# A graph layer on one core: four neighbouring nodes to a partition, and the mixer's projections made in the gather stage

## The chip, the core and the metric

The kernel runs on one core of one Trainium2 chip. The metric is device time in microseconds. The core has five engines that work side by side and wait for one another through semaphores: TensorE (PE in the profile; PEld is its weight load), VectorE (DVE), ScalarE (ACT), GpSimd (POOL) and SyncE (SP), which here only issues DMAs. Each engine takes its instructions in order. GpSimd issues the indirect DMAs that gather table rows.

## The reference

A layer of a graph network over 6250 nodes of 256 features and 206,250 edges, in float32. `xn` is the layer norm of `x`. Three parts follow: graph attention over the edges, a linear-attention mixer over all nodes, and a mixture of eight experts over the normed sum. Cut to what matters here:

```python
xn = _layernorm(x)
# graph attention: x1 = xn @ W, 64 wide; four heads
e = exp(leaky_relu((x1 @ Wl.T)[src] + (x1 @ Wr.T)[dst], 0.2))
w = e / segment_sum(e, src)[src]
gnn = elu(segment_sum(w[:, h] * x1[dst], src) + b)      # for each head h
# mixer: 4 heads of 32
q, k, v = split(rmsnorm(xn, g_pre) @ w_qkv)
k, v = with the 4 memory columns mem_kv put ahead
q = softmax(q, over the 32 of a head) * 32 ** -0.5
k = softmax(k, over all nodes)
mix = rmsnorm((k^T v applied to q) @ w_out + b_out, g_out) + xn
y = x + gnn + mix
out = y + layernorm(y) + sum over the top 2 of 8 experts of gelu(..w1..) w2
```

The softmax of `k` runs over all nodes, so the mixer's small matrix `cw` (`k^T v`, scaled, times `w_out`) is known only when every node's key and value have been seen. Nothing of the mixer enters the graph attention; both meet in `y`.

## The kernel before

Nodes are taken in 49 tiles of 128 (`NT`), the last with 106. Node `128 t + p` lies in tile `t` on partition `p`. Tiles are handled in 13 `groups` of up to four (`GT`). PSUM is shared out in small pools; the ones that matter are `mps` in the first part, and `hps` (one buffer, `h_ps`) and `yps` (two buffers, `y_ps`) later.

**The front.** `load_edges()` (L201) brings the ids of source and destination; lines 244 to 255 cut them into a tile-pair number (`bid`) and two values of a few bits (`va`, `vb`). Then `project()` (L303) is called for each group. It loads four tiles of `x`, takes mean and variance on ScalarE (L309, L315), normalises (L338), transposes on TensorE (L343), copies back (L345) and multiplies with `wcat`, 456 columns: 384 for queries, keys and values, 72 for what the graph attention needs (L348). ScalarE evacuates the product in three pieces: queries to `q_all` (L351), keys and values to `kv` (L352), and the 72 columns to `tab` (L355), which is stored to the DRAM `table`. After each group come three calls of `sort_batch()` (L370), 39 of its 51; it sorts 32 x 128 edges by tile pair with one-hot products, of which the largest operation is the one-hot `ohp` on VectorE (L448). The other 12 batches follow, and between them the steps of `context()` (L467): the maximum of all keys (L468), its spread over the partitions, and for each group a subtraction on GpSimd (L498), an exponential on ScalarE (L499) and one matmul a tile that adds to `ctx_ps` (L502). It ends with `cw` (L521).

**The gather stage.** A loop over blocks of tiles (L1082 and on) does for every tile: `weights()` (L1016), which makes the edges' weights from the gathered rows `xe`; four times `sums()` (L1035), whose one-hot `ohw` (L1041) and matmuls into `a_ps` (L1048) add up a quarter's edges; between them `look()` (L980) for the next tile and a part of `pack()` (L875), which puts a pair of tiles' edges in order and calls `gather()` (L969). That issues 35 indirect DMAs a tile from GpSimd, one a column, into one of three `xe` buffers; a buffer is free again when its tile's sums are done.

**What fills the loop.** Generators in `todo` give up one step at a time. `some_more()` (L1058) is called after each quarter and takes steps until their costs reach `FC` = 2. At first `todo` holds `attention()` (L574): three steps of cost 2 for each group, which turn the queries into the mixer's output and store `base_y`. When it is used up, the experts' weights are loaded, and `finish_steps()` (L661) of each block follows: ELU, norm, routing, and for 8 experts the hidden products (L775), Gelu (L783), the second products (L791) and their weighted addition (L795).

The order of instructions on each engine is laid out by a planner from dependencies and program order. `later()` (L567) adds a dependency, without a semaphore, on the first gather's indices, so that an instruction isn't placed ahead of the gather stage.

The lines of the order in which work is given out:

```python
for t0, n in groups:
    project(t0, n)
    for _ in range(3):
        sort_batch(batches.pop(0))
...
todo = [(attention(), [FC] * (3 * len(groups)))]
```

Of the kernel before, what the change touches and what calls it, by code (L numbers as in the profile page):

```python
# [1 line left out]

# [6 lines left out]
F32 = mybir.dt.float32  # L9
F16 = mybir.dt.float16  # L10
BF16 = mybir.dt.bfloat16
I32 = mybir.dt.int32
# [5 lines left out]
P = 128  # L18
# [17 lines left out]
def tile_gps_layer(  # L36
# [37 lines left out]
    last = N - (NT - 1) * P  # L74
    EC = -(-NE // P)
# [14 lines left out]
    KW = 2 * HID + 1  # L90
    O_TAB = 3 * HID
    O_EL = O_TAB + H + FO
    PW = O_EL + H
    assert NPAD > N and PW <= 512 and last > 0
# [72 lines left out]

    def load_rows(dst_tile, source, t0, n, rows):
        full = n if (t0 + n) * P <= rows else n - 1
        if full < n:  # L170
            nc.vector.memset(dst_tile[:, full, :], 0.0)
        if full:
            nc.sync.dma_start(
                out=dst_tile[:, :full, :],
                in_=source[t0 * P:(t0 + full) * P, :].rearrange("(t p) d -> p t d", p=P),
            )
        if full < n:
            r = rows - (t0 + full) * P
            nc.sync.dma_start(out=dst_tile[:r, full, :], in_=source[(t0 + full) * P:rows, :])
# [21 lines left out]
    def load_edges(pool):  # L201
        return load_ids(pool, "src_i", src, NB * U * P), load_ids(pool, "dst_i", dst, N)
# [33 lines left out]
    with tc.tile_pool(name="ids", bufs=1) as lp:  # L236
# [21 lines left out]
    nc.scalar.dma_start(out=wcat[:, :, :3 * HID], in_=w_qkv.rearrange("(c p) f -> p c f", p=P))  # L258
    nc.scalar.dma_start(
        out=wcat[:, :, O_TAB + H:O_EL], in_=gnn_W.rearrange("(c p) f -> p c f", p=P)  # L260
    )
# [3 lines left out]
    gpre = kp.tile([P, DC], F32, name="gpre")  # L265
# [5 lines left out]
    wo = kp.tile([P, D], F32, name="wo")  # L271
    nc.scalar.dma_start(out=wo, in_=w_out)
    mk = kp.tile([P, NM], F32, name="mk")
    nc.scalar.dma_start(out=mk, in_=mem_kv[0].rearrange("h d m -> (h d) m"))
    mv = kp.tile([P, NM], F32, name="mv")
# [6 lines left out]
    for c in range(DC):  # L282
        wt_ps = mps.tile([FO, P], F32, name="tp")
        nc.tensor.transpose(wt_ps, wcat[:, c, O_TAB + H:O_EL], ident)
        wT = qw.tile([FO, P], F32, name="wT")
        nc.scalar.copy(wT, wt_ps)
        wlr_ps = mps.tile([P, 2 * H], F32, name="pr")
        nc.tensor.matmul(wlr_ps, lhsT=wT, rhs=lrT, start=True, stop=True)
        nc.scalar.copy(wcat[:, c, O_TAB:O_TAB + H], wlr_ps[:, :H])
        nc.scalar.copy(wcat[:, c, O_EL:PW], wlr_ps[:, H:])  # L290
        nc.vector.tensor_scalar(
            wcat[:, c, :3 * HID], wcat[:, c, :3 * HID], gpre[:, c:c + 1], None, op0=OP.mult
        )

    q_all = qp.tile([P, NT, HID], F32, name="q_all")
    kv = kp.tile([P, NT, KW], F32, name="kv")
    nc.gpsimd.memset(kv[:, :, KW - 1:KW], 1.0)
    kmax = kp.tile([P, HID], F32, name="kmax")
# [4 lines left out]
    def project(t0, n):  # L303
# [10 lines left out]
        for j in range(n):  # L314
# [8 lines left out]
        rn = qw.tile([P, GT], F32, name="rn")  # L323
        nc.scalar.activation(rn[:, :n], var, AF.Sqrt, scale=float(D))
        nc.vector.tensor_mul(rn[:, :n], rn[:, :n], rs)
        nc.vector.tensor_scalar_max(rn[:, :n], rn[:, :n], 1e-12)
        nc.vector.reciprocal(rn[:, :n], rn[:, :n])
        nc.vector.tensor_scalar_mul(rn[:, :n], rn[:, :n], float(D) ** 0.5)
        shift = qw.tile([P, GT], F32, name="shift")
        nc.vector.scalar_tensor_tensor(  # L330
            shift[:, :n], stats[:, t0:t0 + n, 0], -1.0, rs, op0=OP.mult, op1=OP.mult
# [3 lines left out]
        for j in range(n):  # L335
# [3 lines left out]
                xn, xt[:, j, :], AF.Identity, bias=shift[:, j:j + 1], scale=rstd[:, t:t + 1]  # L339
# [7 lines left out]
            for c in range(DC):  # L347
# [3 lines left out]
            nc.scalar.activation(q_all[:, t, :], pr[:, :HID], AF.Copy, scale=rn[:, j:j + 1])  # L351
            nc.scalar.activation(  # L352
                kv[:, t, :2 * HID], pr[:, HID:3 * HID], AF.Copy, scale=rn[:, j:j + 1]
            )
            nc.scalar.copy(tab[:, j, :], pr[:, O_TAB:PW])  # L355
        nc.gpsimd.tensor_copy(el[:, t0:t0 + n, :], tab[:, :n, TW - 1:])
        nc.gpsimd.memset(tab[:, :n, TW - 1:TW], 1.0)
        nc.sync.dma_start(
            out=table[t0 * P:(t0 + n) * P, :].rearrange("(t p) f -> p t f", p=P),
            in_=tab[:, :n, :TW],  # L360
        )
# [104 lines left out]

    def context():  # L467
        nc.vector.tensor_reduce(  # L468
            kmax, kv[:, :NT - 1, :HID].rearrange("p t d -> p d t"), axis=AX.X, op=OP.max
        )  # L470
        nc.vector.tensor_max(kmax[:last], kmax[:last], kv[:last, NT - 1, :HID])
        km_ps = mps.tile([HID, P], F32, name="tp")
        nc.tensor.transpose(km_ps, kmax, ident)
        kcol = kp.tile([P, 2], F32, name="kcol")
        nc.vector.tensor_reduce(kcol[:, 0:1], km_ps, axis=AX.X, op=OP.max)
        nc.vector.tensor_reduce(kcol[:, 1:2], mk, axis=AX.X, op=OP.max)
        kmc = kp.tile([P, 1], F32, name="kmc")
        nc.vector.tensor_max(kmc, kcol[:, 0:1], kcol[:, 1:2])
        kr_ps = mps.tile([P, HID], F32, name="tp")
        nc.tensor.transpose(kr_ps, kmc.to_broadcast([P, P]), ident)  # L480
        krow = kp.tile([P, HID], F32, name="krow")
        nc.vector.tensor_copy(krow, kr_ps)
        nkm = kp.tile([P, 1], F32, name="nkm")
        nc.vector.tensor_scalar_mul(nkm, kmc, -1.0)
        emk = kp.tile([P, NM], F32, name="emk")
        nc.scalar.activation(emk, mk, AF.Exp, bias=nkm)
        mm_ps = mps.tile([NM, 2, P], F32, name="tp")
        nc.tensor.transpose(mm_ps[:, 0, :], emk, ident)
        nc.tensor.transpose(mm_ps[:, 1, :], mv, ident)
        memT = kp.tile([NM, 2, P + 1], F32, name="memT")  # L490
        nc.vector.memset(memT, 1.0)
        nc.vector.tensor_copy(memT[:, :, :P], mm_ps)
        ctx_ps = mps.tile([P, HID + 1], F32, name="pr")
        nc.tensor.matmul(ctx_ps, lhsT=memT[:, 0, :P], rhs=memT[:, 1, :], start=True, stop=False)
        yield
        for t0, n in groups:
            kk = kv[:, t0:t0 + n, :HID]
            nc.gpsimd.tensor_sub(kk, kk, krow[:, None, :].to_broadcast([P, n, HID]))  # L498
            nc.scalar.activation(kk, kk, AF.Exp)  # L499
            for t in range(t0, t0 + n):  # L500
                rows = P if t < NT - 1 else last
                nc.tensor.matmul(  # L502
                    ctx_ps, lhsT=kv[:rows, t, :HID], rhs=kv[:rows, t, HID:KW],
                    start=False, stop=(t == NT - 1),
                )
            yield
        rden = kp.tile([P, 1], F32, name="rden")
        nc.vector.reciprocal(rden, ctx_ps[:, HID:HID + 1])
        nc.vector.tensor_scalar_mul(rden, rden, float(DH) ** -0.5)
        cbd = kp.tile([P, HID], F32, name="cbd")  # L510
        nc.vector.memset(cbd, 0.0)
        for h in range(MH):
            s = slice(h * DH, (h + 1) * DH)
            nc.vector.tensor_scalar(cbd[s, s], ctx_ps[s, s], rden[s], None, op0=OP.mult)
        cT_ps = mps.tile([P, HID], F32, name="tp")
        nc.tensor.transpose(cT_ps, cbd, ident)
        cT = kp.tile([P, HID], F32, name="cT")
        nc.scalar.copy(cT, cT_ps)
        cw_ps = mps.tile([P, D], F32, name="pr")
        nc.tensor.matmul(cw_ps, lhsT=cT, rhs=wo, start=True, stop=True)  # L520
        nc.scalar.copy(cw, cw_ps)  # L521
        yield

# [6 lines left out]
    nc.sync.dma_start(out=eltab.rearrange("(t p) h -> p t h", p=P), in_=el)  # L530
# [13 lines left out]
    steps = context()  # L544
    while batches:
        sort_batch(batches.pop(0))
        next(steps, None)
    for _ in steps:
        pass
# [23 lines left out]

    def attention():  # L574
# [4 lines left out]
        for t0, n in groups:  # L579
# [10 lines left out]
            o_g = qw.tile([P, GT, D], F32, name="o_g")  # L590
            ss = qw.tile([P, GT], F32, name="ss")
            for j in range(n):
# [7 lines left out]
                sq = qw.tile([P, D], F32, name="sq")  # L600
# [9 lines left out]
            for j in range(n):  # L610
# [9 lines left out]
            nc.sync.dma_start(  # L620
                out=base_y[t0 * P:(t0 + n) * P, :].rearrange("(t p) d -> p t d", p=P),
                in_=xt[:, :n, :],
            )
# [37 lines left out]
    def finish_steps(hps, yps, x2, t0, n, rows_left, gb, more=None):  # L661
# [8 lines left out]
        def rows_at(t, k):  # L670
            return slice(t * P, (t + k) * P) if isinstance(t, int) else bass.ds(t * P, k * P)

        def front():
            yt = fw.tile([P, GT, D], F32, name="yt")
            nc.sync.dma_start(
                out=yt[:, :n, :],
                in_=base_y[rows_at(t0, n), :].rearrange("(t p) d -> p t d", p=P),
            )
# [121 lines left out]
        def store():  # L800
            full = n if rows_left is None else n - 1
            if full:
                nc.sync.dma_start(
                    out=out[rows_at(t0, full), :].rearrange("(t p) d -> p t d", p=P),
                    in_=x2[:, :full, :],
                )
            if full < n:
                nc.sync.dma_start(out=out[(NT - 1) * P:N, :], in_=x2[:rows_left, n - 1, :])
# [455 lines left out]
```

## Time and profile before

| | us |
|---|---|
| three runs | 4218.44, 4218.94, 4224.91 (median 4218.94) |
| the profiled execution | 4182.5 |
| its span, from first to last instruction | 4180.7 |
| first gather issued | 446.22 |
| last gather issued (last column's start) | 3993.6 |

| engine | busy us | share of the span | instructions |
|---|---|---|---|
| PE | 2268.6 | 54% | 15401 |
| PEld | 1663.9 | 40% | 15401 |
| DVE | 1919.8 | 46% | 3941 |
| ACT | 746.2 | 18% | 1653 |
| POOL | 1669.8 | 40% | 1774 |

How to read the profile's lines: in a row of slices, each digit is the busy share of a fortieth of the span in tenths; PEclk is the granted TensorE clock in tenths. A group of instructions reads: line, engine, operation, output and inputs, shape, count, then busy time in us and mean ns of one, then the engine's idle time just before them and what ended it. A row in order of time reads: start, duration, engine, line, operation, names, count, and in brackets the idle time before it with what ended it. A row of a stretch of time gives its length, then busy time and count for PE, PEld, DVE, ACT and POOL, the granted clock as a share of one, the share of the DMA engines and GB/s. A wait ended by "remote" is one whose end the profile can't put down to an instruction.

### The profile page before, as it was taken

What the parts mean: (1) busy time and instruction counts of PE and PEld (TensorE: products, weight loads), DVE (VectorE), ACT (ScalarE), POOL (GpSimd) and SP (SyncE); (2) the same over time, 40 slices, a digit from 0 to 9 for tenths busy, and PEclk for the clock granted to TensorE, in tenths of its full rate; (3) what the DMA queues carried; (4) which work ended last, traced back from release to release, by engine and by line L of the source; (5) the groups of instructions that cost most, each with busy time, mean ns of one, the idle gap of its engine ahead of it and who ended that gap; (6) DMA issues with size and microseconds to landing.
All of it is one profiled execution on the core that took longest, in us unless ns stands there. A gap on an engine that the chain in (4) does not pass through costs nothing. (4 is left out here: it accounts for less than half of the span.)

```text
span 4180.7 us, 39357 instructions
## 1 busy us (share of the span) xinstructions
PE 2268.6 (54%) x15401; PEld 1663.9 (40%) x15401; DVE 1919.8 (46%) x3941; ACT 746.2 (18%) x1653; POOL 1669.8 (40%) x1774
## 2 busy tenths in 40 slices
PE   7877232435254764644765555455364573554677
PEld 4544232324242543433543433334253352442456
DVE  7787444536352443533442523425343452342423
ACT  5542001212111111111111110111111111110122
POOL 1001545454445344344344344544535335344410
PEclk8875555666666877776877776777676686776778
DMA  1020111111121111011011100101101001011100
GB/s 59 28 29 1 21 28 41 37 41 37 34 74 20 22 19 23 18 24 22 12 29 18 25 17 17 30 17 22 25 12 27 18 19 25 13 25 19 23 12 7
DMA packets 106548, 103.75 MB, mean 25 GB/s; under 512 B 42678, under 2 KB 78740, under 8 KB 106356
## 3 DMA queue, kind: packets, MB, share of 16 engines
q0 software_dynamic: 54720, 60.52, 8.4%
q1 hardware_dynamic: 49940, 39.75, 3.3%
q8 instruction: 123, 2.02, 0.2%
q10 hardware_dynamic: 1696, 0.89, 0.1%
q14 instruction: 69, 0.57, 0.0%
HBM read 86.39 MB, written 14.65 MB: 24 GB/s over the span
## 5 line engine op out<-in xcount | busy, mean ns | idle before, releaser
L972 POOL DMA_INDIRECT xe<-table,dst_x x1710 | 1635.7, 957 | 2011.0 <-PE a_ps L1048 1323.2
L1048 PE MATMUL a_ps<-ohw,xe 128*65 128x128 f32 x4400 | 665.1, 307 | 235.7 <-issue 189.3
L1048 PEld LDWEIGHTS a_ps<-ohw,xe 128*65 128x65 f32 x4400 | 590.8, 159 | 314.4 <-issue 243.1
L775 PE MATMUL h_ps<-tokT,w1s 128*128 128x512 f32 (+3 forms) x896 | 442.8, 610 | 235.1 <-ACT hT L783 205.1
L795 DVE SCALAR_TENSOR_TENSOR x<-y_ps,comb,x 128x256 f32<-128x256 f32 x392 | 187.0, 481 | 782.4 <-remote 479.1
L791 PE MATMUL y_ps<-w2s,hT 128*128 128x256 f32 x1568 | 436.7, 413 | 147.6 <-issue 107.2
L791 PEld LDWEIGHTS y_ps<-w2s,hT 128*128 128x128 f32 x1568 | 315.5, 208 | 273.0 <-issue 177.5
L940 PE MATMUL s_ps<-rc,ohp 128*128 128x144 f16 x2525 | 255.1, 260 | 279.5 <-DVE ohp L935 146.8
L1041 DVE TENSOR_TENSOR ohw<-oh,bank 128x1280 f32<-128x1280 bf16 x196 | 321.5, 1641 | 170.1 <-remote 149.3
L940 PEld LDWEIGHTS <-ohp 128*128 128x128 f16 x2525 | 209.6, 114 | 324.2 <-DVE ohp L935 162.9
L1009 PE MATMUL e_ps<-elw,ohT 128*128 128x48 bf16 x588 | 36.2, 199 | 544.7 <-ACT ohT L1001 477.8
L783 ACT ACTIVATE hT<-h_ps,b1s 128x512 f32<-128x512 f32 (+3 forms) x224 | 140.4, 627 | 1018.4 <-remote 531.0
L775 PEld LDWEIGHTS h_ps<-tokT,w1s 128*128 128x128 f32 x896 | 171.8, 214 | 345.7 <-ACT hT L783 226.0
L1001 ACT COPY ohT<-t_ps 128x768 bf16<-128x768 bf16 x98 | 78.3, 799 | 1130.1 <-remote 842.3
L930 DVE TENSOR_TENSOR rc<-ohc,bank 128x1152 f16<-128x1152 f16 (+1 forms) x350 | 231.2, 687 | 64.8 <-remote 62.2
L1009 PEld LDWEIGHTS <-ohT 128*128 128x128 bf16 x588 | 27.0, 106 | 577.2 <-ACT ohT L1001 505.9
L935 DVE TENSOR_TENSOR ohp<-to,bank 128x2048 f16<-128x2048 f16 (+1 forms) x175 | 193.5, 1105 | 0.0
L763 PE MATMUL y_ps<-b2s,cTs 8*128 8x256 f32 x98 | 49.7, 600 | 192.4 <-ACT cTs L761 118.6
L764 DVE TENSOR_TENSOR x<-x,y_ps 128x256 f32<-128x256 f32 x49 | 20.6, 420 | 269.7 <-remote 164.6
L1018 DVE TENSOR_REDUCE z<-e_ps 128x140 f32<-128x420 f32 (+1 forms) x49 | 28.7, 585 | 244.6 <-PE e_ps L1009 224.1
L923 DVE TENSOR_TENSOR ohc<-to,bank 128x1152 f16<-128x1152 f16 (+1 forms) x175 | 119.6, 683 | 0.3 <-ACT to L911 0.2
L448 DVE TENSOR_TENSOR ohp<-rank,iota_h 128x4096 f16<-128x4096 f16 (+1 forms) x51 | 116.1, 2277 | 6.3 <-ACT rank L439 6.0
(273 smaller groups left out, 2568.0 us busy)
## 6 DMA issues: line engine op xcount, KB each, us to landing
xe<-table,dst_x POOLq DMA_INDIRECT x1710
xt<-in_x_dram SPq DMA_DIRECT2D x24, 512.0 KB
base_y<-xt SPq DMA_DIRECT2D x12, 512.0 KB
yt<-base_y SPq DMA_DIRECT2D x9, 512.0 KB
out_dram<-x SPq DMA_DIRECT2D x9, 512.0 KB
w1s<-in_L_ffn_w_dram SPq DMA_DIRECT2D x8, 256.0 KB
w2s<-in_L_ffn_w_dram SPq DMA_DIRECT2D x8, 256.0 KB
table<-tab SPq DMA_DIRECT2D x12, 138.0 KB
```

The costliest lines, as they stand in the source:

```text
L448: nc.vector.tensor_tensor(pairs(ohp[:, :w]), two(rank2[:, :w], P // 2), row(iota_h, P // 2), op=OP.is_equal)
L775: nc.tensor.matmul(h_ps[:, :w], lhsT=w1s[:, e, c, f * P:(f + 1) * P], rhs=held["tokT"][:, c, :w], start=(c == 0), stop=(c == DC - 1),)
L783: nc.scalar.activation(held[e][:, f, :w], h_ps[:, :w], AF.Gelu, bias=b1s[:, k:k + 1])
L791: nc.tensor.matmul(y_ps, lhsT=held[e][:, f, j * P:(j + 1) * P], rhs=w2s[:, e, f, :], start=(f == 0), stop=(f == FC - 1),)
L795: results.append(nc.vector.scalar_tensor_tensor(x2[:, j, :], y_ps, held["comb"][:, j, e:e + 1], x2[:, j, :], op0=OP.mult, op1=OP.add,))
L923: nc.vector.tensor_tensor(pairs(ohc[:, :m]), twos(to[:, 0, t0:t0 + m], U * CW // 2), iota_2[:, :, :U * CW // 2].to_broadcast([P, m, U * CW ...
L930: nc.vector.tensor_tensor(pairs(rc[:, :m, i, :]), pairs(ohc[:, :m]), twos(edges_q[:, t0:t0 + m, i, :], U * CW // 2), op=OP.mult,)
L935: nc.vector.tensor_tensor(pairs(ohp[:, :m]), twos(to[:, 1, t0:t0 + m], P // 2), iota_2.to_broadcast([P, m, P // 2, 2]), op=OP.is_equal,)
L940: nc.tensor.matmul(flat(s_ps), lhsT=ohp[:, t - t0, :], rhs=flat(rc[:, t - t0]), start=(t == 0), stop=(t == NBT - 1),)
L972: nc.gpsimd.indirect_dma_start(out=xe[:, c, :], out_offset=None, in_=table, in_offset=bass.IndirectOffsetOnAxis(ap=dst_x[:, c:c + 1], axis=0),
L1041: nc.vector.tensor_tensor(ohw[:, :n], oh[:, g0:g1, i, None, :].to_broadcast([P, n, H, SN]), ew_s[:, c0:c0 + n, :, None].to_broadcast([P, n ...
L1048: nc.tensor.matmul(a_ps[:, i].rearrange("f h n -> f (h n)"), lhsT=xe[:, c, H:], rhs=ohw[:, c - c0].rearrange("p h n -> p (h n)"), start=(c ...
```

## The change

Two things are done at once.

**The layout.** Of the first 48 tiles (`NF`), four make a block of 512 nodes, and node `512 g + 4 p + t` now lies on partition `p` of tile `4 g + t`: four neighbouring nodes share a partition, one in each of four tiles. The last tile stays as it was. `pieces()` gives the matching views of a DRAM tensor, and `load_rows()` and a new `store_rows()` use it for `x`, `table`, `base_y` and `out`; a group of four tiles is then one run of four rows in DRAM for each partition. The source ids are renumbered to fit in `load_edges()`, with five VectorE operations over 128 x 1612. The tables in DRAM keep the nodes' order, so the destination ids and the gathers' indices stay as they are.

**The projections.** `project()` keeps only the 72 columns for the graph attention; it also keeps the norm's scale and shift of every tile in `rn_all` and `shift_all`. Queries, keys and values move to a new `context()`, a generator in `todo` ahead of `attention()`. For each group it loads `x` again, normalises with both norms' factors in one ScalarE operation, transposes, and projects: the keys transposed, 128 x 512 for four tiles, the queries and values a tile at a time. In place of one maximum over all nodes it holds a running one: a single number a feature, raised group by group, and `sums_c` is shrunk by `exp(old - new)` before a group's `k^T v` is added. The costs of the steps become 1 each, 80 in all. Some buffers of `attention()` go from two to one (`o_g`, `sq`). The store of `eltab`, which only the overflow branch at the end reads, moves into that branch.

The diff, cut to its core:

```diff
+    NF = N // (GT * P) * GT
+    def pieces(dram, t0, n, rows):
...
+            if t < NF:
+                e = min(t0 + n, g + GT)
+                ap = dram[g * P:(g + GT) * P, :].rearrange("(p t) f -> p t f", t=GT)
+                found.append((t - t0, e - t0, P, ap[:, t - g:e - g, :]))
...
     def load_edges(pool):
-        return load_ids(pool, "src_i", src, NB * U * P), load_ids(pool, "dst_i", dst, N)
+        src_i, dst_i = load_ids(pool, "src_i", src, NB * U * P), load_ids(pool, "dst_i", dst, N)
...
+        nc.vector.scalar_tensor_tensor(
+            part, src_i, float(NF * P), src_i, op0=OP.is_lt, op1=OP.mult
+        )
+        nc.vector.tensor_single_scalar(turn, part, GT - 1, op=OP.bitwise_and)
+        nc.vector.tensor_scalar(
+            part, part, 2, P - 1, op0=OP.logical_shift_right, op1=OP.bitwise_and
+        )
+        nc.vector.scalar_tensor_tensor(
+            src_i, turn, float(P - 1), src_i, op0=OP.mult, op1=OP.add
+        )
+        nc.vector.scalar_tensor_tensor(
+            src_i, part, -float(GT - 1), src_i, op0=OP.mult, op1=OP.add
+        )
...
     def project(t0, n):
...
-            nc.scalar.activation(q_all[:, t, :], pr[:, :HID], AF.Copy, scale=rn[:, j:j + 1])
-            nc.scalar.activation(
-                kv[:, t, :2 * HID], pr[:, HID:3 * HID], AF.Copy, scale=rn[:, j:j + 1]
-            )
-            nc.scalar.copy(tab[:, j, :], pr[:, O_TAB:PW])
+            nc.scalar.copy(tab[:, j, :], pr)
...
-    steps = context()
     while batches:
         sort_batch(batches.pop(0))
-        next(steps, None)
...
+    def context():
...
+        xt = load(0)
+        yield
+        for g, (t0, n) in enumerate(groups):
+            v = vs[g % 2]
+            xnT = qw.tile([P, DC, GT * P], F32, name="xnT", bufs=1)
+            for j in range(n):
+                t = t0 + j
+                xn = xn_of()
+                nc.scalar.activation(
+                    xn, xt[:, j, :], AF.Identity, bias=shift_all[:, t:t + 1],
+                    scale=rn_all[:, t:t + 1],
+                )
+                xT_ps = yps.tile([P, DC, P], F32, name="y_ps")
+                for c in range(DC):
+                    nc.tensor.transpose(xT_ps[:, c, :], xn[:, c * P:(c + 1) * P], ident)
+                nc.scalar.copy(xnT[:, :, j * P:(j + 1) * P], xT_ps)
+            if g + 1 < len(groups):
+                xt = load(g + 1)
+            yield
...
+            k_ps = hps.tile([P, GT * P], F32, name="h_ps")
+            for c in range(DC):
+                nc.tensor.matmul(
+                    k_ps[:, :w], lhsT=wqvk[:, c, 2], rhs=xnT[:, c, :w],
+                    start=(c == 0), stop=(c == DC - 1),
+                )
+            here = small("here")
+            nc.vector.tensor_reduce(here, k_ps[:, :w], axis=AX.X, op=OP.max)
+            new = small("most")
+            nc.vector.tensor_max(new, most, here)
+            less = small("less")
+            nc.vector.tensor_scalar_mul(less, new, -1.0)
+            shrink = small("shrink")
+            nc.scalar.activation(shrink, most, AF.Exp, bias=less)
+            most = new
+            ekT = qw.tile([P, GT * P], F32, name="ekT", bufs=1)
+            nc.scalar.activation(ekT[:, :w], k_ps[:, :w], AF.Exp, bias=less)
+            for j in range(n):
+                qv_ps = yps.tile([P, 2, HID], F32, name="y_ps")
+                for c in range(DC):
+                    nc.tensor.matmul(
+                        flat(qv_ps), lhsT=xnT[:, c, j * P:(j + 1) * P],
+                        rhs=flat(wqvk[:, c, :2]), start=(c == 0), stop=(c == DC - 1),
+                    )
+                nc.scalar.copy(q_all[:, t0 + j, :], qv_ps[:, 0])
+                nc.scalar.copy(v[:, j, :HID], qv_ps[:, 1])
+            yield
+            ek_ps = yps.tile([P, GT, P], F32, name="y_ps")
...
+                nc.tensor.transpose(ek_ps[:r, j, :], ekT[:, j * P:j * P + r], ident)
...
+            nc.scalar.copy(ek[:r, :n], ek_ps[:r, :n])
+            c_ps = yps.tile([P, HID + 1], F32, name="y_ps")
+            for j in range(n):
+                nc.tensor.matmul(
+                    c_ps, lhsT=ek[:r, j, :], rhs=v[:r, j, :], start=(j == 0), stop=(j == n - 1)
+                )
+            nc.vector.scalar_tensor_tensor(
+                sums_c, sums_c, shrink, c_ps, op0=OP.mult, op1=OP.add
+            )
+            yield
...
-    todo = [(attention(), [FC] * (3 * len(groups)))]
+    todo = [(chain(context(), attention()), [1] * (6 * len(groups) + 2))]
```

## The prediction

> **What bounds the kernel now.** I read the page first, then the groups of instructions by line (shapes kept apart), the order of time inside one gather, and last a table of busy time by stretch. On the page, these rows count:
>
> ```profile
> PE   7877232435254764644765555455364573554677
> POOL 1001545454445344344344344544535335344410
> PEclk8875555666666877776877776777676686776778
> L972 POOL DMA_INDIRECT xe<-table,dst_x x1710 | 1635.7, 957 | 2011.0 <-PE a_ps L1048 1323.2 <-issue 595.6 <-PE y_ps L594 57.8
> ```
>
> No engine is full after the first tenth. GpSimd gathers 1710 columns at 957 ns and otherwise waits, mostly for `a_ps`: the sums of a node tile free the `xe` buffer that the next gather writes. A gather is 35 columns, one each 1.25 us (starts 3592.22, 3593.47), so about 44 us; 49 of them are 2140 us of the 4181. A node tile takes longer than that, and the order of time says why:
>
> ```profile
> 3604.23 0.69 PE L791 MATMUL y_ps<-w2s,hT 128*128 128x256 f32 x2 [0.34 <-issue]
> 3604.73 0.94 POOL L972 DMA_INDIRECT xe<-table,dst_x  x1 [0.30 <-issue]
> ...
> 3634.73 0.95 POOL L972 DMA_INDIRECT xe<-table,dst_x  x1 [0.30 <-issue]
> 3641.49 0.58 ACT L783 ACTIVATE hT<-h_ps,b1s 128x384 f32<-128x384 f32 x1 [44.30 <-remote]
> 3641.49 0.48 DVE L795 SCALAR_TENSOR_TENSOR x<-y_ps,comb,x 128x256 f32<-128x256 f32 x1 [30.11 <-remote]
> 3642.13 1.65 PE L775 MATMUL h_ps<-tokT,w1s 128*128 128x384 f32 x2 [37.21 <-ACT hT L783]
> ```
>
> The gather began at 3592.22. For some 12 us the other engines work beside it; then ScalarE waits 44.3 us and VectorE 30.1 us for products that TensorE had finished by 3605, and all go on some 6 us after the last column was issued. So the later two thirds of a gather hide hardly any work that passes between engines. What a tile needs beyond those first 12 us stands behind the gather. The first part of the kernel, before any gather (first at 446.22), is another matter:
>
> ```profile
> L448 DVE TENSOR_TENSOR ohp<-rank,iota_h 128x4096 f16<-128x4096 f16 x50 | 115.2, 2303 | 6.1 <-ACT rank L439 6.0
> L348 PE MATMUL pr<-wcat,xT 128*128 128x456 f32 x196 | 109.8, 690 | 5.9 <-ACT xT L345 5.9
> L468 DVE TENSOR_REDUCE kmax<-kv 128x128 f32<-128x6144 f32 x1 | 11.0, 11044 | 0.0
> ```
>
> ```profile
> core 0: us, PE busy (x) PEld busy (x) DVE busy (x) ACT busy (x) POOL busy (x), PEclk, DMA share, GB/s
> ...
> 200.00:250.00 50.00, 43.92 (x482) 25.57 (x482) 38.30 (x61) 29.16 (x111) 0.61 (x4) 0.77 0.09 28
> 350.00:400.00 50.00, 36.62 (x516) 26.31 (x516) 39.14 (x55) 5.85 (x28) 0.00 (x0) 0.57 0.01 1
> ...
> 558.78:1238.70 679.92, 271.68 (x1852) 223.99 (x1851) 330.97 (x690) 101.19 (x234) 339.98 (x351) 0.64 0.18 41
> 1238.70:1774.90 536.20, 315.21 (x1786) 222.61 (x1784) 238.22 (x513) 89.33 (x132) 234.16 (x245) 0.75 0.12 25
> 2018.80:3201.30 1182.50, 635.10 (x3739) 468.51 (x3738) 479.77 (x1002) 155.59 (x229) 534.70 (x561) 0.72 0.11 21
> ```
>
> While project() runs (200 to 250), TensorE is busy 88% and paces the sort; where sorting is alone (350 to 400), VectorE leads at 78%. The last three rows go from gather start to gather start: 10 tiles with attention as their extra work, 7 with the experts' backlog, 16 in steady state.
>
> **An exchange rate.** Per tile they last 68.0, 76.6 and 73.9 us, with PE, DVE and ACT busy 70.4, 91.8 and 79.4 us in sum. From the first row to the second, 21.4 us more work cost 8.6 us, a rate of 0.40; to the third, 9.0 us cost 5.9, a rate of 0.65. I price work moved into the gather stage so.
>
> **Front, removed.** `pr` shrinks from 456 to 72 columns, two ACT evacuations a tile go (L351 0.364, L352 0.467 us), three small DVE operations a group, the 11.0 us `kmax`, the GpSimd subtraction, the exponential and 98 context matmuls. None of this is on the path by itself: the sort's 51 batches are. Their L448 start at 36.6 and end with 410.0, 50 steps of 7.47 us. With sorting alone (377.77, 384.69, 391.61, 398.53) a step is 6.92. I take that pace for all: 50 x 0.55 = 28 us won. Ends: VectorE's own work in a batch is 6.05 us (L448 2.30, L427 1.02, L444 1.21, L387 0.62, L412 0.59, L399 0.27), with the loop's small operations 6.45, which wins 51; a lighter but still interleaved project() at 7.4 wins 4.
>
> The row shows 0.77 granted clock with project() and 0.57 without, at 88% and 73% TensorE. The Trainium skill, "TensorE: Matmul & The Clock Gate", section "Part 1: The HAM clock gate", says that the array idles at half clock and only sustained work opens it; so thinning TensorE's work would take back part of the gain. By that rule the pace stays at the 6.92 of the half-clock stretch, 28 us; by a clock held at 0.77, up to 51.
>
> **Front, added.** load_edges() renumbers the source nodes: three scalar_tensor_tensor over 128x1612 (L252, 1.83 us) and two tensor_scalar (L248, 1.00), 7.5 us on VectorE between the arrival of the indices (6.4 us) and the first batch. Nothing hides it but TensorE's first projections, which get shorter too: +7.5, ends 0 and 7.5.
>
> **Gather stage, added.** Each group of four tiles now needs, by the nearest rows (busy time over count). On PE, 4 matmuls of 512 columns (L775, 0.494) for keys, 16 of 256 (L791, 0.279) for queries and values, 12 transposes (L343, 0.247), 8 of 129 (L502, 0.186): 2.0 + 4.5 + 3.0 + 1.5 = 11.0 us. On ACT, 4 normalisations (L338, 0.606), 4 copies (L345, 0.385), the shrink factor (0.30, as L321), the exponential (0.634, as L499), 8 copies of queries and values (0.264, as L596), the copy of `ek` (0.58, as L1106): 7.6 us. On DVE, a maximum over 512 (0.68, as L583), two small ones (0.15 each), the update of `sums_c` (0.29, as L482): 1.3 us.
>
> That is 19.9 us, times 12.25 groups (49 tiles) 244 us. At 0.40 it costs 98 us; at 0.65, 158. I take 0.40, the rate of the busiest stretch, since these tiles are as loaded. The lower end is 0, if the gathers hide it after all.
>
> Where the work falls: two cost units a call and one a step now, so 80 steps in 40 calls; tiles 0 to 5 carry 2.7 groups of context each, tiles 5 to 10 2.7 of attention where there were 1.3. The total of attention is unchanged, and the experts start at the same tile; at one rate this moves nothing, and the other rate is in the range. The waits it adds are ACT's for `y_ps` (two buffers, shared with heads and experts). Queued behind them on ACT are the `ohT` copies of look(), on which TensorE's `e_ps`, then `z` and the next tile's sums wait.
>
> **DMAs.** 13 more loads of x on SP (0.37 us to issue), each a group ahead of its use, covered by two more steps; without that cover a load would be seen in full, as the 8 us from 7.17 to the first use at 15.36. Nothing is added on GpSimd's queue. The `eltab` store moves behind a branch not taken: 0, SP was idle. Four rows to a partition make longer pieces of x, base_y, table and out. None of these transfers is on the path; they can only slow a gather's columns, whose mean is 957 ns against 944 undisturbed: 1710 x 13 ns = 22 us at most to win, and with 13 loads more on some 37, 8 to lose. I take 0.
>
> **Sum.** -28 + 7.5 + 98 = +78 us on the profiled 4182.5 (span 4180.7): 4260. The three runs shown have a median of 4218.94, 36 above the profiled one; I carry the difference over: 4297 us, slower by 1.8%. Its own range, from the ends: 98 - 51 + 0 - 22 = +25 to 158 - 4 + 7.5 + 8 = +170, so 4244 to 4389.
>
> **The rivals**, each with its time at the level of the median.
>
> **The gathers hide it.** The change's 244 us run inside the idle two thirds of the gathers, at no price: 4219 - 28 + 7.5 = 4198, faster. For it: TensorE is at 40% in the first ten tiles, and now and then it does run a whole quarter of sums late in a gather. Against: the stall at 3605, and that attention's work already shows in the period. It decides if less than 20 of the 244 us shows. Chance 0.19.
>
> **Handing over is what costs.** A group passes 16 times between TensorE and ScalarE where attention passes 8 times, and each passage that falls into a gather may wait for its end. At 0.65 or above: 4219 - 20 + 158 = 4357; at 1.0, 4443. For it: in the view of waits, ScalarE's `ohT` copies stand 842 us in all. Against: the heaviest stretch has the lower rate. Chance 0.20.
>
> **It doesn't move.** The planner could draw the projections back into the front; then TensorE, at 88%, pays again and only 7.5 us is sure: about 4226 and up. Against: the added gates let nothing begin before the first gather's indices. Chance 0.03.
>
> **It cancels** to within the noise, with a gather price near 20 us: 4219. Chance 0.05.
>
> **How the numbers follow.** The forecast holds 0.53, and 4297 is its value. Slower by over 0.2%: 0.53 + 0.20 + 0.03, less 0.01 that ends level = 0.75. Within 0.2% (8 us, about what a measurement of this kernel can tell from no change): 0.06. Faster: 0.19. The range 4190 to 4395 takes in the likeliest's own range, the level cases, most of the first rival and half of the second; 0.10 is left out on either side.
>
> **What would show it.** Right: the first gather starts near 426 instead of 446; the L448 of the new kernel step at 6.9; tiles 0 to 5 last some 80 us instead of 68; from tile 11 on the periods are as before. Wrong: a front no shorter (then the sort's own chain paces it), a first gather before 400, tiles 0 to 5 still at 70 (the first rival), or at 95 and more (the second). A change of the period in steady state would mean that the layout matters, which I cost at nothing.

## The result, and the profile after

The changed kernel takes 4261.89 us (median of 4, 4255.28 to 4272.14) beside 4220.51 us before: ratio 1.0106, 95% interval 1.0087 to 1.0126. It is slower by 41 us; 78 were forecast. The profiled execution is one of the four (4272.14 us). That of before (4182.5) lay 38 us under its median, so the two profiles are compared by place, not by their ends.

Rows of the page of the changed kernel, the same as were shown of before:

```profile
PE   6876244644344666464655554455364473554577
POOL 1000654454545334435344345444535335344410
PEclk9999567767676777686777776777677686776778
...
L1043 POOL DMA_INDIRECT xe<-table,dst_x x1710 | 1631.1, 954 | 2143.1 <-PE a_ps L1119 1426.4
```

A column still takes 954 ns (957 before); GpSimd waits 1426 us for the sums, where it waited 1323. The first gather starts at 425.6 us (446.22 before). The one-hots of the sort (now L474) start at 38.8 and the last one at 389.4: 50 steps of 7.01 us, where they were 7.47. The table of busy time by stretch, from gather start to gather start (to 0.1 us), the same tiles as the three rows shown of before:

```profile
541.10:1274.40 733.30, 348.90 (x2309) 278.29 (x2309) 336.76 (x716) 153.90 (x442) 337.41 (x351) 0.70 0.16 41
1274.40:1834.70 560.30, 322.23 (x1776) 228.31 (x1777) 249.13 (x550) 90.53 (x138) 232.39 (x246) 0.72 0.14 31
2070.40:3275.60 1205.20, 634.01 (x3763) 467.46 (x3762) 482.36 (x1006) 158.29 (x232) 535.36 (x561) 0.72 0.10 20
```

Counted from 0, tiles 2 to 11 last 53 us longer, with 136 us more work on PE, DVE and ACT; the next seven 24 longer with 19 us more, and the 16 steady ones 23 longer with 4 us more. What the context costs the engines, from the groups of instructions between 425 and 1300 us (line, engine, operation, count, then busy us and mean ns):

```profile
L620 PE MATMUL y_ps<-wqvk,xnT 128*128 128x256 f32 x196 | 59.9, 447 | 95.4 <-remote 51.1 <-ACT v L625 37.1 <-ACT xnT L595 6.5
L588 ACT ACTIVATE xn<-xt,shift_all,rn_all 128x256 f32<-128x256 f32 x49 | 28.8, 603 | 0.0
L602 PE MATMUL h_ps<-xnT,wqvk 128*128 128x512 f32 (+1 forms) x52 | 28.0, 649 | 1.6 <-ACT xnT L595 1.6
L595 ACT COPY xnT<-y_ps 128x256 f32<-128x256 f32 x49 | 17.7, 372 | 62.0 <-remote 31.1 <-PE y_ps L594 19.2 <-issue 8.5
```

With its other rows (L594, L637 and L631 on PE, L613 to L634 on ACT, L607 to L640 on DVE) it is 137 us on PE, 93 on ACT and 17 on DVE: 247 in all, where the prediction had counted 244.

### The profile page after: what moved, and what is told of

It is laid out like the page before. It is cut to its first block, busy times and chain, and to the rows that moved or that the text cites. A ratio compares the mean times of both kernels' runs of the same rounds, so it can differ in the third digit from the quotient of the medians.

```text
span 4270.3 us, 40363 instructions
## 1 busy us (share of the span) xinstructions
PE 2346.3 (55%) x15794; PEld 1734.3 (41%) x15794; DVE 1921.4 (45%) x3951; ACT 767.0 (18%) x1763; POOL 1653.5 (39%) x1760
## 4 chain that ended last, share of the span: by engine, by line
another core or an unknown queue 28%; PE 27%; DVE 6%; issue 5%; ACT 2%; DVEq 0%; ACTq 0%
PE y_ps L869 7%; PE a_ps L1119 7%; PE h_ps L853 7%; PE s_ps L1011 2%; PE y_ps L841 1%; DVE ohw L1112 1%; ACT hT L861 1%; PE y_ps L790 1%; DVE ohp L1006 1%; DVE rc L1001 1%; PE t_ps L1068 1%; DVE inc L964 1%; ACT ohT L1072 0%; DVE x L873 0%
## 5 line engine op out<-in xcount | busy, mean ns | idle before, releaser
L1119 PE MATMUL a_ps<-ohw,xe 128*65 128x128 f32 x4400 | 632.0, 298 | 157.1 <-issue 86.9
L1119 PEld LDWEIGHTS a_ps<-ohw,xe 128*65 128x65 f32 x4400 | 566.8, 154 | 219.7 <-issue 122.5
L869 PE MATMUL y_ps<-w2s,hT 128*128 128x256 f32 x1568 | 445.9, 419 | 142.9 <-issue 127.1
L842 DVE TENSOR_TENSOR x<-x,y_ps 128x256 f32<-128x256 f32 x49 | 20.6, 420 | 280.8 <-PE y_ps L841 160.4
L474 DVE TENSOR_TENSOR ohp<-rank,iota_h 128x4096 f16<-128x4096 f16 (+1 forms) x51 | 115.2, 2258 | 14.6 <-ACT rank L465 14.5
```

The source lines that it names most:

```text
L474: nc.vector.tensor_tensor(pairs(ohp[:, :w]), two(rank2[:, :w], P // 2), row(iota_h, P // 2), op=OP.is_equal)
L869: nc.tensor.matmul(y_ps, lhsT=held[e][:, f, j * P:(j + 1) * P], rhs=w2s[:, e, f, :], start=(f == 0), stop=(f == FC - 1),)
L1119: nc.tensor.matmul(a_ps[:, i].rearrange("f h n -> f (h n)"), lhsT=xe[:, c, H:], rhs=ohw[:, c - c0].rearrange("p h n -> p (h n)"), start=(c ...
```

## The experiments

**One thing has to be known first.** The experiments were run in five series, each on one chip and each with the kernel before beside it. That kernel showed two levels: 2741 us in three series (on chips 9, 12 and 12), 4186 to 4188 us in two (on chips 12 and 0). Every run of a series stood at one level, and chip 12 showed both. The 4220 of the result belongs to the upper one, and so does the profile of before (4182.5). So ratios are read within a series, and each effect has a level.

**e1: the kernel before, again.** No edit.

> The kernel before, once more, for a profile beside the others of this call. The profiled execution of before lay 36 us under the median of its runs, that of the changed kernel 10 us over its own. Theory 1 (the 36 us are one execution's luck): the median is 4219 again, the profile's span lies within 15 us of it, and the 16 steady tiles that lasted 73.9 us each last about 75.2, as they do in the changed kernel (75.3). Theory 2 (the layout or the moved work lengthens the steady tiles by 1.4 us): they last 73.9 again.

2741.23 us, ratio 1.0001 (0.9991 to 1.0010) to the runs of before beside it, and 1480 us under the 4220 of the result. Neither theory had this. From its page and its view of waits (line, what it waited for, us in total, times, longest):

```profile
POOL 1000203777777777777777777777777777777710
...
L972 POOL DMA_INDIRECT xe<-table,dst_x x1710 | 1648.4, 964 | 619.2 <-issue 602.7
```

```profile
POOL xe L972 <- issue: 602.7, 1656, 98.5
ACT hT L783 <- PE h_ps L775: 447.7, 187, 9.4
ACT ohT L1001 <- PE t_ps L997: 367.0, 92, 25.9
```

And the view of waits of before, as profiled for the prediction:

```profile
POOL xe L972 <- PE a_ps L1048: 1323.2, 44, 51.4
ACT ohT L1001 <- remote: 842.3, 37, 45.1
...
ACT hT L783 <- remote: 531.0, 18, 44.3
DVE x L795 <- remote: 479.1, 25, 34.4
```

It is the same program with the same 39357 instructions and the same 1.25 us a column. At the lower level there is not one wait ended by "remote"; at the upper one VectorE and ScalarE have 129 that last 2633 us in all. In e1, without them, the sums are done in time, GpSimd never waits for a buffer, and all 1710 columns go out back to back, the first at 444.6 and the last at 2612.7 us. There the time is the start of the first gather, plus 2168 us, plus a tail of 126. I call the levels "in bursts" and "back to back".

**e2 and e11: the layout alone**, in the kernel before: the renumbering with its five operations, and the new views for `x`, `table`, `base_y` and `out`.

```diff
     def load_edges(pool):
...
+        nc.vector.scalar_tensor_tensor(
+            src_i, turn, float(P - 1), src_i, op0=OP.mult, op1=OP.add
+        )
...
-                out=yt[:, :n, :],
-                in_=base_y[rows_at(t0, n), :].rearrange("(t p) d -> p t d", p=P),
+            load_rows(yt, base_y, t0, n, NPAD)
```

> The layout alone: four neighbouring nodes on a partition and the renumbering of the sources, with projections and context left in the front as before. Theory 1 (prediction): only the renumbering counts, +7.5 us (0 to 7.5) before the first batch of the sort, nothing in the gather stage: 4219 to 4228, ratio 1.000 to 1.002. Theory 2 (the layout changes the gather stage, at 1.4 us a tile): +40 to +75, ratio 1.01 to 1.018. Below 4210 would mean that the longer pieces help.

> The layout alone once more, wanted on a chip whose gathers come in bursts, since the first run of it was on one where they run back to back (+4.9 us). There: only the renumbering, +2 to +8, ratio 1.000 to 1.002, if the doubled attention of the run before is what costs the 23 us; +15 to +25, ratio 1.0035 to 1.006, if the layout is. Back to back: 1.0017 again.

Both came back to back: 1.0017 (1.0008 to 1.0026) and 1.0019 (1.0010 to 1.0028), +4.9 and +4.8 us; the first gather of e2 starts at 449.0, that of e1 at 444.6. Within the noise that is the renumbering and nothing else. In bursts the layout was not seen alone.

**e3: the move alone**, the changed kernel with the rows' views and `load_edges()` as before, and **e4: the changed kernel without its context**, where each group's work in `context()` gives way to three steps and the queries are set to zero:

```diff
-                ap = dram[g * P:(g + GT) * P, :].rearrange("(p t) f -> p t f", t=GT)
+            found.append((0, full, P, dram[a:a + full * P, :].rearrange("(t p) f -> p t f", p=P)))
```

```diff
-            v = vs[g % 2]
-            xnT = qw.tile([P, DC, GT * P], F32, name="xnT", bufs=1)
...
+            yield
+            yield
+            later(nc.vector.memset(q_all[:, t0:t0 + n, :], 0.0))
+            yield
```

> The move alone: projections and context in the gather stage with the running maximum, rows laid out as before, no renumbering. Theory 1: the changed kernel's 4262 less the renumbering: 4254 (4250 to 4262), and a first gather near 418. Theory 2 (the layout makes the loss): 4190 to 4215.

> The changed kernel without the 13 groups of context in the gather stage (their loads of x, projections, exponentials and sums are left out, queries are set to zero; the calls and their order stay). It measures the price of the moved 247 us (137 on TensorE, 93 on ScalarE, 17 on VectorE by the changed kernel's rows). Theory 1 with my rate of 0.40: 4262 - 99 = 4163. With the rate that the medians imply (41 + 20 = 61 us over 247: 0.25): 4201. Rival, the gathers hide it and something else costs: 4240 to 4262. The first gather stays near 426 in all of these.

Back to back: 2718.57 us, 0.9916 (0.9903 to 0.9930), and 2717.53 us, 0.9915 (0.9901 to 0.9929). The move wins 22 us, the first gather starting at 420.3 in place of 444.6. The two kernels differ by the context and also by the layout, which e4 has (its first gather starts at 425.7) and e3 has not. With the 4.9 us of e2 for the layout, the 247 us of context cost about 6 us; against the whole change (e5 below, another series) they cost 2. Theory and numbers were made for bursts; here the rival holds: the gathers hide nearly all of it.

**e5: the changed kernel again**, and **e6: its context done twice.**

```diff
+          for rep in range(2):
+            sums_z = sums_c if rep else sums_b
             xnT = qw.tile([P, DC, GT * P], F32, name="xnT", bufs=1)
...
-                sums_c, sums_c, shrink, c_ps, op0=OP.mult, op1=OP.add
+                sums_z, sums_z, shrink, c_ps, op0=OP.mult, op1=OP.add
...
-    todo = [(chain(context(), attention()), [1] * (6 * len(groups) + 2))]
+    todo = [(chain(context(), attention()), [1] + [0, 1] * (3 * len(groups)) + [1] * (3 * len(groups) + 1))]
```

The last line lets the doubled steps fall on the same calls of `some_more()` as the single ones.

> The changed kernel again, beside the runs of before of the same chip. Theory 1: the sign depends on whether the other engines' signals stand while GpSimd issues a gather. Where they do (a kernel before of 4219 us, gathers in bursts of 35 columns with pauses) 4262, ratio 1.010; where they don't (a kernel before of 2741 us, 1710 columns back to back) only the front counts: 2741 - 22 (what the move alone won there) + 5 (what the layout alone cost) = 2724, ratio 0.994. Rival (the call's runs differ by something else than the gathers): the ratio is not tied to the level of the time.

> The changed kernel with every group's context done twice (a first pass into sums of its own that nothing reads, then the real one, from the same load of x): another 13 groups, some 240 us of work more in the same calls. Where the gathers come in bursts it measures the rate at the margin: at 0.25 us per us, 4262 + 60 = 4322; at 0.40, 4358; at 1, 4502; if the gathers hide it, 4262. Where they run back to back (before 2741): TensorE is 70% busy from 424 to 1000 us, so 135 us more of it would fill that stretch; 2724 if what is left hides it, 2740 to 2800 if TensorE becomes the bound there.

Back to back again: 2719.55 us for the changed kernel, 0.9932 (0.9913 to 0.9951). The same change that is 1.1% slower in bursts is 0.7% faster here; the 2724 foretold from e2 and e3 were 4 too many. The second context costs 28 us (2747.47, ratio to before 1.0028, 1.0018 to 1.0038), inside the 2740 to 2800 expected if TensorE became the bound. GpSimd now waits 31.5 us for `a_ps`, which it didn't in e5. Busy time by stretch, e5 and then e6 (columns as before: length; PE, PEld, DVE, ACT, POOL; clock; DMA; GB/s):

```profile
425.40:1000.00 574.60, 399.57 (x2842) 320.21 (x2843) 438.73 (x951) 185.53 (x506) 438.50 (x447) 0.82 0.31 69
```

```profile
424.80:1000.00 575.20, 464.75 (x3216) 372.73 (x3217) 439.20 (x963) 251.16 (x727) 415.99 (x426) 0.88 0.30 68
```

TensorE goes from 70% to 81% of that stretch and GpSimd's columns from 447 to 426. The cover is finite: the first 247 us are nearly free, the next cost a ninth of themselves.

**e7, e8, e9: gather and sums made to take turns**, by one buffer for the gathered rows: the kernel before, the changed one, and the changed one without context (as e4).

```diff
-        xe = gw.tile([P, CPT, TW], F32, name="xe", bufs=3)
+        xe = gw.tile([P, CPT, TW], F32, name="xe", bufs=1)
```

> The kernel before with one buffer for the gathered rows in place of three, so that a node tile's gather can't begin until the sums of the tile before it have read that buffer: bursts of 35 columns with pauses, made by the buffers alone. Where the gathers otherwise run back to back (before 2741 us) a tile should take some 44 us of gather and 25 to 40 us of sums behind it: 3700 to 4500 us. It is the base for the next two. Where they come in bursts anyway (before 4219) 4300 to 5000.

> The changed kernel with one such buffer. Theory S (it is enough for a price that gather and sums take turns, since the moved work then stands in the pause): 20 to 80 us slower than the kernel before with one buffer, ratio 1.005 to 1.02, as on record with three buffers. Theory F (the price needs signals that stand during a gather; where they don't, the gather hides the moved work even when it takes turns): 15 to 22 us faster, ratio 0.994 to 0.996.

> The changed kernel with one such buffer and without the 13 groups of context (loads, projections, exponentials and sums left out, queries zero). Against the run before it: theory S: the 247 us of context are worth 40 to 100 us (a rate of 0.16 to 0.40); theory F: 0 to 15 us.

This series came in bursts (before 4186.41 us, three buffers), so theory F couldn't be tried. But the runs measure the price there: 4250.43, 4297.50 and 4255.09 us. One buffer costs the kernel before 64 us; its 4250 lie below the 4300 to 5000 expected for bursts. The changed kernel is 47 us slower than before with one buffer as well (1.011 by the medians, where the result has 1.0106), inside theory S's 20 to 80, and the pair is of one series. The context is worth 42 us of it; theory S's bounds for that were 40 to 100. Stretches of e7, e8 and e9, each from the first gather to the start of tile 5's, from there to that of tile 11's, and on to that of the last tile's (to 0.4 us), the tiles counted from 0:

```profile
444.20:823.20 379.00, 148.74 (x1082) 118.21 (x1082) 226.44 (x461) 60.66 (x146) 172.28 (x176) 0.62 0.18 36
823.20:1240.00 416.80, 153.11 (x1169) 123.83 (x1170) 189.44 (x394) 56.87 (x128) 201.09 (x210) 0.66 0.20 42
1240.00:4142.10 2902.10, 1580.55 (x8912) 1133.14 (x8909) 1151.32 (x2431) 400.63 (x605) 1224.73 (x1296) 0.73 0.12 20
```

```profile
425.80:833.80 408.00, 230.09 (x1495) 174.31 (x1495) 203.48 (x415) 103.33 (x279) 168.80 (x176) 0.76 0.16 32
833.80:1271.90 438.10, 189.90 (x1228) 144.44 (x1229) 226.16 (x506) 80.92 (x219) 205.22 (x211) 0.63 0.23 56
1271.90:4193.10 2921.20, 1602.70 (x8941) 1147.20 (x8938) 1153.63 (x2440) 405.64 (x613) 1229.05 (x1296) 0.73 0.12 20
```

```profile
426.10:795.00 368.90, 115.31 (x1002) 101.72 (x1002) 195.42 (x385) 26.03 (x45) 168.49 (x176) 0.71 0.12 17
795.00:1231.40 436.40, 186.81 (x1226) 142.84 (x1227) 224.36 (x495) 80.57 (x218) 205.16 (x211) 0.64 0.23 57
1231.40:4149.30 2917.90, 1594.39 (x8943) 1141.96 (x8940) 1154.14 (x2440) 405.70 (x613) 1224.59 (x1296) 0.73 0.12 20
```

Between the last two kernels it is mainly the first stretch that differs: 39 us for 200 us more on PE, DVE and ACT, a rate of 0.20; the later starts stay 39 to 44 us apart. But e9 is 5 us slower than e7 with no context in its loop and a first gather 18 us sooner. It wins 10 us more in the first stretch, which attention has left, loses 20 in the second, where attention stands twice as thick, and 16 after it. That was not in my sum.

**e10 and e12: attention moved alone**, in the kernel before, to the calls where the changed kernel has it.

```diff
-    todo = [(attention(), [FC] * (3 * len(groups)))]
+    todo = [(hold(), [1] * (3 * len(groups) + 2)), (attention(), [1] * (3 * len(groups)))]
```

Here `hold()` only yields, 41 times; the experts' weights are still loaded only after attention.

> The kernel before, front, layout and projections untouched, with attention moved alone: 41 empty steps before its 39 steps and two steps in a call in place of one, so that it falls on tiles 5 to 10, where the changed kernel has it. Prediction: this is worth nothing. With one buffer, on a chip whose gathers come in bursts, the changed kernel without its context was 5 us slower than before though its first gather began 18 us sooner; if the doubled attention is what costs those 23 us, +10 to +25 (ratio 1.002 to 1.006) where the gathers come in bursts (before 4186 or 4219), and 0 where they run back to back (before 2741). Rival (the layout costs it): ratio 0.999 to 1.001.

> Attention moved alone, once more, wanted on a chip whose gathers come in bursts. There (before 4186 or 4219): +10 to +25, ratio 1.002 to 1.006, if the doubled attention costs the 23 us; 0.999 to 1.001 if the layout does. Back to back (before 2741): 1.0015 again.

Back to back (e10): 1.0015 (1.0006 to 1.0024), +3.6 us where 0 was expected. In bursts (e12): 4203.48 beside 4187.70 us, 1.0036 (1.0024 to 1.0047), +16 us, so moving attention has a price, inside the foretold 10 to 25. Stretches of the kernel before as profiled for the prediction (another series, 5 us from the median of before in this one), and of e12, over the same columns (tiles 0 to 7, 8 to 13, and on to the last tile's start):

```profile
446.20:959.20 513.00, 184.50 (x1253) 150.10 (x1253) 230.41 (x471) 66.04 (x157) 271.16 (x280) 0.61 0.16 34
959.20:1392.00 432.80, 201.34 (x1249) 156.60 (x1250) 206.82 (x456) 72.31 (x141) 202.89 (x211) 0.68 0.17 40
1392.00:3957.30 2565.30, 1381.52 (x8116) 1017.22 (x8114) 1056.09 (x2254) 362.22 (x538) 1133.32 (x1190) 0.72 0.11 21
```

```profile
444.50:928.10 483.60, 159.49 (x1179) 133.01 (x1179) 189.83 (x364) 28.00 (x59) 266.97 (x280) 0.62 0.15 21
928.10:1399.40 471.30, 216.77 (x1298) 165.44 (x1299) 244.80 (x559) 96.16 (x227) 204.48 (x210) 0.68 0.22 53
1399.40:3972.50 2573.10, 1389.10 (x8140) 1020.98 (x8138) 1058.43 (x2258) 365.26 (x541) 1131.77 (x1190) 0.72 0.13 21
```

Taking 104 us of work out of the first stretch wins 29 us (0.28); putting 77 us onto the second costs 38 (0.50), and the rest is 8 us longer. The total of attention is unchanged; here thicker costs more than thinner wins.

## Why the prediction was right in sign and too large

**The bound** held for the level on record: GpSimd waits for sums, and engines stand late in each gather. "Hardly any work that passes between engines" was too strong even there. In the gather that I showed, which began at 3592.22, a one-hot of VectorE runs 17 us later, after one of the "remote" waits and with columns still going out:

```profile
3609.22 1.75 DVE L1041 TENSOR_TENSOR ohw<-oh,bank 128x1536 f32<-128x1536 bf16 x1 [9.66 <-remote]
```

And I took the bound as the kernel's nature. It is a condition under which the kernel ran: the same program ran without it on chips 9 and 12.

**The front** was -28 + 7.5 = -20.5 us, and the first gather came 20.6 us sooner. That agreement is partly luck. Two errors work against each other: a step of the sort is 7.01, not 6.92, so 22.7 were won in place of 28; and of the 7.5 us of renumbering only 2 to 4 showed at the first one-hot (38.8 after 36.6 in the two profiles, 39.1 after 34.7 in e2 and e1, 38.8 after 34.8 in e4 and e3). In the pairs of one series (e1 and e4, e7 and e8, e7 and e9) the first gather comes 18.9, 18.8 and 18.4 us sooner. (The end of 51 us rests on a sum of 6.05 us whose terms give 6.01.) The clock played no part, though I weighed it. The front of one and the same kernel, in the changed kernel's first profile and then in e5:

```profile
200.00:250.00 50.00, 42.52 (x552) 28.99 (x549) 36.89 (x53) 22.24 (x90) 2.59 (x4) 1.00 0.09 28
```

```profile
200.00:250.00 50.00, 42.51 (x550) 28.91 (x547) 36.89 (x53) 22.24 (x90) 2.59 (x4) 0.50 0.10 28
```

At a granted clock of 1.00 and 0.50 the busy times are equal, the transposes (L376) have a median of 421 ns in both between 100 and 350 us, the sort's steps are 7.01 and 7.00 us, and the first gather starts at 425.6 and 425.5. The Trainium skill, "TensorE: Matmul & The Clock Gate", section "Part 1: The HAM clock gate", has sustained work open the clock, and warns that the clock's records in a trace can be unreliable. Here TensorE was 85% busy in both rows, and one of them shows half clock. Whether that record is wrong or this work doesn't depend on the clock isn't shown; either way the recorded clock doesn't tell the pace of this front.

**The gather stage** is the step that failed: 98 us, "at 0.40". The work was sized right (247 for 244), the rate was not. Measured, the context costs 42 us in bursts with one buffer (0.17 over all of it). I had read the rate from two stretches that differ in what they do, attention in one and experts in the other, and applied it everywhere. The pairs that change only the work give 0.20 for context on tiles cleared of attention, 0.28 for attention taken away and 0.50 for attention thickened (the last two from profiles of two series): no one rate fits all three, and the highest is found where a tile already carries attention. Whether context is cheap because of where it stands, or because it is work of TensorE and ScalarE and not of VectorE, wasn't told apart.

**Attention doubled on a tile**, which I put at 0 with "at one rate this moves nothing", is 16 us (e12). By the runs the sum is -19 + 42 + 16 = +39, beside 41 on record; that is closer than the parts are known, since e12 alone has an interval of 10 to 20 us and the result one of 37 to 53. The layout's DMAs, at 0, agree back to back; in bursts they were not seen alone. With one buffer, e9 is 23 us slower than e7 once its earlier start is taken off; e12's 16 leave 7 us of that, to be shared by the layout, the single buffers of attention (`o_g`, `sq`) and noise. None of these was tried alone in bursts, so they stay open.

**What would show it.** Starts near 426 and steps near 6.9: yes. Tiles 2 to 5 last 74.5 us each ((839.0 - 541.0) / 4) for the 80 foretold, 65.4 before; all six from tile 0 on last 68.9, and 62.4 before where I had written 68, since tile 0 lasts 44 to 45 us in both kernels. So "still at 70" would have spoken for the first rival, and was badly chosen as a sign. "From tile 11 on as before" fails by 1.4 us a tile in the two profiles, in the 16 steady tiles. In e7 and e8, of one series, the rest from there lasts 2902.1 and 2921.2 us, 19 us more (0.5 a tile), and 16 of these are in e9 too, so they aren't the context's. Part may be attention's, since e12, with attention moved alone, has a rest 8 us longer than the profile of before. The cause is open.

**The rivals.** "The gathers hide it" (0.19) is right back to back, where the front counts and the change wins 0.7%, and wrong in bursts. "Handing over is what costs" asked for a rate of 0.65 or above; the highest measured is 0.50, and that for attention. "It doesn't move" is out: the context's rows above stand in the gather stage.

None of these kernels is the fastest at both levels. In bursts before is the fastest tried; back to back the move alone (2718.57) and the whole change (2719.55, another series) can't be told apart, and both beat before.

## What to carry to other kernels

Before pricing moved work, ask what makes the stage's engines stand, and whether it belongs to the program or to the conditions of that execution: here a second profile of the same kernel, taken at the other level, would have shown it before the forecast. Price a move by both its ends, the place it leaves and the place it thickens, since a rate drawn from averages over different stages is not one that work can be traded at. And the part that starts an unbroken chain (here the first gather) was worth its full time back to back: 24 us sooner in e3, 22 us won. In bursts it was seen only as a term of a sum that fits.

## What the hardware showed that was not expected

The same program took 2741 and 4187 us with the same instructions and 1.25 us a column at both. What the traces show beside it is 2633 us of waits (summed over VectorE and ScalarE) whose end the profile can't put down to an instruction. By time some two thirds of them end 3 to 6 us after the end of a gather's last column (60 waits, 1727 us), but another 60, with 695 us, end while columns still go out. What sets the level wasn't found: it changed between series on one chip, never within one.

The granted clock that the profile gives for a stretch differed by a factor of two between executions of one kernel (1.00 and 0.50), with equal busy times there.
